# Two small operations of an expert mixture change engines, and its queue of steps starts two steps further on

## The chip, the cores and the metric

The kernel runs on one core of a Trainium2 chip. Its time is the device time of one execution in microseconds (us); of the kernel before, ten executions took 3360.54 to 3378.72 us, and their median, 3370.7 us, is the number that the change is held against. Every engine (PE for matrix products, DVE the vector engine, ACT the scalar engine, POOL the GpSimd engine, SP which only issues transfers) works through its own instructions strictly in the order in which they were written, and engines wait for one another on semaphores.

## What is computed

Two transformer layers over x of shape 4 x 1024 x 128 (four rows of 1024 tokens), float32. The first layer adds two attentions to x; it is not touched by the change. The second layer, cut to what matters:

```python
xn = _layernorm(x)
# linear (random feature) attention, one row of 1024 tokens at a time
x = x + attn(xn) \
# mixture of 8 experts, top 2 of them for each token, and one shared expert for all tokens
for e in range(8):
    h = gelu(xf @ w1[e] + b1[e])               # 128 -> 512
    out = out + combine[:, e:e+1] * (h @ w2[e] + b2[e])
shared = gelu(xf @ ws1 + bs1) @ ws2 + bs2
x + (out + shared)
```

`combine` holds, for each token, the two weights of the softmax over its two best experts.

## The kernel before

**The second layer's stage.** It begins at 2893 us of the execution and lasts to the end, 470 us. It has four strands of work, written as Python generators whose pieces are put one behind the other by a driver loop (line 1811 on):

- *The attention of a row*: `favor_keys(b)` and `favor_queries(b)`, for row b = 0 to 3. In each pass of the loop one piece of each running generator is written. There are 20 passes with the keys of row 0, then three times 40 passes with the queries of one row and the keys of the next, then 20 with the queries of row 3.
- *aside*, the last row's own way into the mixture (`last_row`, line 1350): the layernorm of row 3 (line 215), the router, the tables of blocks, and 16 scatters by POOL (line 1343) that send row 3's tokens, 128 at a time, to their experts' slots in `sorted_x` in HBM. Rows 0 to 2 did this during the first layer.
- *The shared expert* (`shared`, line 1653), in chunks of 512 tokens, 8 in all. One chunk is two pieces. In the first piece: four products `ph` with `ws1` (line 1693) and their Gelu on ACT (line 1697), then the transpose `yT` of the chunk ahead (line 1681), added to x by DVE. In the second: `cT` (line 1660), `py` with `ws2` (line 1669) and with the biases (line 1672).
- *The experts* (`experts`, line 1706): 39 blocks of 256 slots, j = 0 to 38. SP loads the block's rows `xg` from `sorted_x` and its weights `w1`, `w2` (three buffers each). PE transposes the rows (`xgT`, line 1728), DVE copies them out of PSUM (line 1730). `whose` is a copy of the two numbers that ride behind each row, its token's number and its weight (line 1732). PE multiplies by `w1` (`pb`, line 1740), ACT takes the Gelu (`hb`, line 1746), PE multiplies by `w2` (`pe`, line 1755). The result is multiplied by the slot's weight into `yb` (line 1761), and POOL adds it to the tokens' rows of two sums in HBM, by an indirect transfer (line 1765).

The shared expert's first six chunks, then the rest of *aside*, then the experts, then the shared expert's last two chunks make one generator, `fill`. The driver takes a piece of *fill* by a clock of its own: `due` grows by a rate in each pass (0.84 in the first 20, then 0.5, at last 1.2), and for each whole 1 in it a piece of *fill* is written. Two pieces are one chunk of the shared expert or one block of the experts. *aside* gets three pieces of every pass at first, then two, so that it has run dry before *fill* comes to it.

```python
for _ in run(*its):
    for _ in range(3 if taken < 15 else 2):
        next(aside, None); taken += 1
    due += rate
    while due >= 1.0:
        due -= 1.0
        next(filler, None)
```

PE and SP keep the order in which the pieces are written. DVE, ACT and POOL are put in order by the framework's scheduler in this stage.

**The end.** When the last block's sums have landed, SP loads both sums (`y`, 16 transfers of 256 KB, line 1832), DVE adds them to x (line 1836), and eight transfers of 256 KB take x out (line 1838).

Of the kernel before, what the change touches and what calls it, by code (L numbers as in the profile page):

```python
# [12 lines left out]
AF = mybir.ActivationFunctionType  # L13
ALU = mybir.AluOpType
# [4 lines left out]
B, T, D = 4, 1024, 128  # L19
# [42 lines left out]
ROW = D + 2  # L62
# [9 lines left out]
def two_layers(ctx: ExitStack, tc: tile.TileContext, a: dict, out: bass.AP):  # L72
    nc = tc.nc
# [12 lines left out]
    def small(name):  # L86
        return banks.tile([P, 512], F32, tag="small", name=name)
# [1618 lines left out]
    def experts():  # L1706
        rows_of = sorted_x.rearrange("(k q p) d -> k p q d", q=MB // P, p=P)
        loaded, seconds, turned, hidden, whose = {}, {}, {}, {}, {}

        def load(j):  # L1710
            at = nc.sync.value_load(block[0:1, 1, j : j + 1], min_val=0, max_val=ME * PER)
            xg = ff.tile([P, MB // P, ROW], F32, tag="xg", name=f"xg{j}", bufs=3)
            nc.sync.dma_start(xg, rows_of[ds(at, 1)].rearrange("o p q d -> p (o q) d"))
            e = nc.sync.value_load(block[0:1, 0, j : j + 1], min_val=0, max_val=ME - 1)
            w1 = ff.tile([P, MH], F32, tag="w1", name=f"w1_{j}", bufs=3)
            nc.sync.dma_start(w1, a["w1"][ds(e, 1)].rearrange("o d m -> d (o m)"))
            loaded[j] = xg, w1

        def load_second(j):
            e = nc.sync.value_load(block[0:1, 0, j : j + 1], min_val=0, max_val=ME - 1)  # L1720
            w2 = ff.tile([P, MHC, D], F32, tag="w2", name=f"w2_{j}", bufs=3)
            nc.sync.dma_start(w2, a["w2"][ds(e, 1)].rearrange("o (c p) d -> p (o c) d", p=P))
            seconds[j] = w2

        def turn(j):
            pt = small(f"xgT{j}")
            for q in range(MB // P):
                nc.tensor.transpose(pt[:, ts(q, P)], loaded[j][0][:, q, 0:D], ident)  # L1728
            turned[j] = ff.tile([P, MB], F32, tag="xgT", name=f"xgT{j}")
            nc.vector.tensor_copy(turned[j], pt[:, 0:MB])  # L1730
            whose[j] = ff.tile([P, MB // P, 2], F32, tag="whose", name=f"whose{j}", bufs=6)
            nc.gpsimd.tensor_copy(whose[j], loaded[j][0][:, :, D:ROW])

        def one(j):
            w1, xT = loaded.pop(j)[1], turned.pop(j)
            hT = hidden[j] = ff.tile([P, MHC, MB], F32, tag="hb", name=f"hb{j}")
            for c2 in range(MHC // 2):
                ph = small(f"pb{j}_{c2}")
                for k in range(2):
                    nc.tensor.matmul(  # L1740
                        ph[:, ts(k, MB)], lhsT=w1[:, ts(2 * c2 + k, P)], rhs=xT,
                        start=True, stop=True,
                    )
                for k in range(2):
                    c = 2 * c2 + k
                    nc.scalar.activation(
                        hT[:, c, :], ph[:, ts(k, MB)], AF.Gelu, bias=b1s[:, j, c : c + 1]
                    )

        def two(j):  # L1750
            w2, hT, to = seconds.pop(j), hidden.pop(j), whose.pop(j)
            py = small(f"pe{j}")
            for q in range(MB // P):
                for c in range(MHC):
                    nc.tensor.matmul(  # L1755
                        py[:, ts(q, D)], lhsT=hT[:, c, ts(q, P)], rhs=w2[:, c, :],
                        start=(c == 0), stop=(c == MHC - 1),
                    )
            yb = ff.tile([P, MB // P, D], F32, tag="yb", name=f"yb{j}", bufs=3)
            for q in range(MB // P):  # L1760
                nc.vector.tensor_scalar(
                    yb[:, q, :], py[:, ts(q, D)], to[:, q, 1:2], None, ALU.mult
                )

                nc.gpsimd.indirect_dma_start(
                    out=sums[q][:, :],
                    out_offset=bass.IndirectOffsetOnAxis(
                        ap=to[:, q, 0:1].bitcast(I32), axis=0
                    ),
                    in_=yb[:, q, :], in_offset=None, compute_op=ALU.add,  # L1770
                )

        for j in range(NBLK + 3):
            if j < NBLK:
                load(j)
            if 0 <= j - 1 < NBLK:
                turn(j - 1)
            if 0 <= j - 1 < NBLK:
                load_second(j - 1)
            if 0 <= j - 2 < NBLK:  # L1780
                one(j - 2)
                yield
            if 0 <= j - 3 < NBLK:
                two(j - 3)
                yield
# [13 lines left out]
    def fill():  # L1799

        yield from shared(0, SOON)
        for _ in aside:
            pass
        yield from experts()
        yield from shared(SOON, B * T // TC)

    filler = fill()
    due, taken = 0.0, 0
    for k, (rows_now, rate) in enumerate((
        ((0,), 0.84), ((0, 1), 0.5), ((1, 2), 0.5), ((2, 3), 0.5), ((3,), 1.2),  # L1810
    )):
# [88 lines left out]
```

## Time and profile before

| what | value |
|---|---|
| ten runs, median (lowest to highest) | 3370.7 us (3360.54 to 3378.72) |
| the profiled execution, its own time | 3365.59 us |
| its span, from first to last instruction | 3363.8 us |
| mean granted clock of PE over the span | 0.974 |
| busy in the span: PE, DVE, ACT, POOL | 94%, 72%, 55%, 56% |
| `yb` (line 1761), DVE, 78 instructions | 24.1 us |
| `whose` (line 1732), POOL, 39 instructions | 28.8 us |
| loads of ACT's function tables for Exp and Gelu at lines 1392, 1746 and 1697 | 31, 32 and 5, 1283 ns each |

The profiled execution is one of the faster ones: it took 5.1 us less than the median. Times below are in microseconds from the start of its span. In the views a line reads: start, duration, engine, line of the kernel, operation, output <- inputs, shapes, how many instructions were merged, and in brackets how long the engine had been idle and what ended that. PEld is PE's loading of the stationary operand, SPq is SP's queue of transfers.

### The profile page before, as it was taken

To read this page: it belongs to the slowest core of one execution; us is meant where nothing else is said; L and a number is where in the kernel's file an instruction comes from. 1 tells how busy PE (TensorE), PEld (TensorE's weight loads), DVE (VectorE), ACT (ScalarE), POOL (GpSimd) and SP (SyncE) were. 2 spreads that over 40 slices of the span, in tenths; PEclk is the share of its full clock that TensorE was granted. 3 is DMA by queue.
4 is the path that set the end of the run, shared out by engine and by line. 5 is a ranking of instruction groups with operands and counts; after the bars stand their busy time and mean duration, and the time that the engine had idled before them with its cause. 6 is when DMAs were issued, how large, how long until landed. Compare 5 with 4: busy or idle time off the path is not lost. (4 is left out here: it accounts for less than half of the span.)

```text
span 3363.8 us, 48933 instructions
## 1 busy us (share of the span) xinstructions
PE 3172.1 (94%) x15323; PEld 1716.4 (51%) x15323; DVE 2418.7 (72%) x4670; ACT 1850.9 (55%) x3273; POOL 1894.0 (56%) x2345
## 2 busy tenths in 40 slices
PE   6889999999999999999899999999999999889998
PEld 3344444555545444455454455455455554457776
DVE  6787786767778867666867786667666654658886
ACT  3345555555555555555555555555556566246665
POOL 2455555666557666665476666665767654123333
PEclk8899999999999999999999999999999999889999
DMA  5124443433322323333233232332333220024446
GB/s 154 35 82 132 132 140 104 120 101 91 92 69 78 93 80 93 90 93 88 61 91 90 86 94 84 92 89 80 96 90 94 82 84 15 12 62 89 86 88 134
DMA packets 458696, 299.77 MB, mean 89 GB/s; under 512 B 42490, under 2 KB 431108, under 8 KB 458436
## 3 DMA queue, kind: packets, MB, share of 16 engines
q1 hardware_dynamic: 412692, 225.32, 23.9%
q0 software_dynamic: 42976, 70.26, 8.0%
q8 instruction: 122, 2.00, 0.2%
q10 hardware_dynamic: 2768, 1.07, 0.1%
q14 instruction: 138, 1.13, 0.1%
HBM read 179.83 MB, written 116.26 MB: 88 GB/s over the span
## 5 line engine op out<-in xcount | busy, mean ns | idle before, releaser
L620 DVE TENSOR_REDUCE nmh<-mx 128x1 f32<-128x512 f32 x1024 | 664.0, 680 | 293.4 <-PE mx L614 201.4
L874 POOL DMA_INDIRECT sorted_v<-xv,gates x464 | 461.8, 995 | 334.8 <-DMA sorted_v<-xv,gates 249.5
L675 ACT ACTIVATE pT<-sT 128x512 f32<-128x512 f32 x1024 | 557.8, 600 | 162.6 <-PE sT L668 67.5
L955 DVE TENSOR_REDUCE nms<-ps 128x1 f32<-128x1024 f32 x256 | 310.6, 1213 | 259.4 <-ACT ps L953 249.1
L950 PE MATMUL ss<-xnT,qTs 128*128 128x512 f32 x1024 | 491.7, 602 | 3.9 <-ACT qTs L820 2.3
L826 POOL TENSOR_TENSOR g_o<-g_o 128x256 f32<-128x256 f32 x256 | 191.5, 748 | 513.2 <-DVE g_o L825 484.4
L1003 PE MATMUL po<-ow,cTs 128*128 128x512 f32 x1024 | 476.9, 598 | 2.4 <-DVE nmh L620 1.6
L982 PE MATMUL cp<-pTs,vs 128*128 128x512 f32 x1024 | 458.5, 601 | 18.2 <-DVE pTs L974 9.8
L953 ACT COPY ps<-ss 128x512 f32<-128x512 f32 x512 | 298.6, 588 | 216.5 <-PE ss L950 183.9
L957 ACT ACTIVATE ps<-ps,nms 128x1024 f32<-128x1024 f32 x256 | 294.5, 1150 | 146.6 <-DVE nms L955 122.8
L1007 DVE TENSOR_TENSOR g_o<-po,go 128x512 f32<-128x512 f32 x512 | 332.7, 680 | 38.9 <-PE po L1003 18.5
L614 PE MATMUL mx<-ks,qs 72*128 72x512 bf16 x1024 | 313.4, 383 | 17.1 <-DVE nmh L620 7.1
L668 PE MATMUL sT<-qs,ks 75*128 75x512 bf16 x1024 | 311.4, 384 | 8.6 <-DVE nmh L620 3.0
L982 PEld LDWEIGHTS cp<-pTs,vs 128*128 128x128 f32 x1024 | 192.0, 192 | 242.5 <-issue 226.6
L970 PE MATMUL pTp<-ident,ps 128*128 128x128 f32 x2048 | 275.8, 278 | 21.4 <-ACT ps L957 8.8
L970 PEld LDWEIGHTS pTp<-ident,ps 128*128 128x128 f32 x2048 | 243.8, 143 | 90.3 <-issue 21.1
L950 PEld LDWEIGHTS ss<-xnT,qTs 128*128 128x128 f32 x1024 | 189.5, 191 | 183.2 <-issue 108.6
L926 POOL DMA_INDIRECT vs<-yv,gates x232 | 229.0, 987 | 67.5 <-issue 59.7
L926 POOL DMA_INDIRECT yg<-yv,gates x232 | 224.6, 968 | 73.7 <-issue 73.4
L1003 PEld LDWEIGHTS po<-ow,cTs 128*128 128x128 f32 x1024 | 180.0, 192 | 162.8 <-issue 133.7
L987 ACT COPY cTs<-cp 128x512 f32<-128x512 f32 x64 | 37.5, 586 | 392.2 <-PE cp L982 312.6
L658 PE MATMUL ov<-pT,va 128*32 128x512 f32 x2048 | 249.2, 604 | 0.0
(321 smaller groups left out, 4827.1 us busy)
## 6 DMA issues: line engine op xcount, KB each, us to landing
vb<-in_v_w_dram SPq DMA_DIRECT2D x667, 64.0 KB
xs<-sorted_v SPq DMA_DIRECT2D x145, 256.0 KB
yv<-xs SPq DMA_DIRECT2D x145, 256.0 KB
w<-in_w_dram SPq DMA_DIRECT2D x78, 256.0 KB
sorted_x<-nobody SPq DMA_DIRECT2D x16, 1040.0 KB
ow<-in_o_w_dram SPq DMA_DIRECT2D x32, 512.0 KB
qs<-qd SPq DMA_DIRECT2D x144, 64.0 KB
sorted_v<-xv,gates POOLq DMA_INDIRECT x464
```

The costliest lines, as they stand in the source:

```text
L614: nc.tensor.matmul(sc, lhsT=qs[0:NPAIR, i, ts(n, P)], rhs=ks[0:NPAIR, ts(kc, 512)], start=True, stop=True,)
L620: nc.vector.tensor_reduce(halves[:, i, n, kc : kc + 1], sc, axis=AX.X, op=ALU.max)
L668: nc.tensor.matmul(sc, lhsT=ks[:, ts(kt, P)], rhs=qs[:, i, ts(c, 512)], start=True, stop=True,)
L675: nc.scalar.activation(pT, sc, AF.Exp)
L874: nc.gpsimd.indirect_dma_start(out=sorted_v[u % 4][:, :], out_offset=bass.IndirectOffsetOnAxis(ap=column(u, k, n).bitcast(I32), axis=0), i ...
L926: nc.gpsimd.indirect_dma_start(out=to[:, n, :], out_offset=None, in_=unit[u, "y"][:, :], in_offset=bass.IndirectOffsetOnAxis(ap=column(u, ...
L950: nc.tensor.matmul(sc, lhsT=qT[:, ts(n, P)], rhs=xnT[b][:, ts(c, 512)], start=True, stop=True)
L955: nc.vector.tensor_reduce(nm, p, axis=AX.X, op=ALU.max, negate=True)
L970: nc.tensor.transpose(pt[:, ts(k, P)], p[:, ts(4 * k4 + k, P)], ident)
L982: nc.tensor.matmul(cp, lhsT=v[:, kt, :], rhs=pT[:, kt, :], start=(kt == 0), stop=(kt == NT - 1),)
L1003: nc.tensor.matmul(po, lhsT=cT[:, ts(qt, P)], rhs=unit[u, "ow"][:, ts(c, 512)], start=True, stop=True,)
L1007: nc.vector.tensor_tensor(g[:, ts(c, 4), :], po.rearrange("p (e c) -> p e c", e=4), bcast(go[:, ts(c, 4)], P), ALU.mult,)
```

## The change

`whose` is copied by DVE instead of POOL; the product with the slots' weights is made by ACT (a Copy with a scale read from memory, one per partition) instead of DVE; and the driver's clock starts at 2.0 instead of 0.0.

```diff
@@ turn(j)
-            nc.gpsimd.tensor_copy(whose[j], loaded[j][0][:, :, D:ROW])
+            nc.vector.tensor_copy(whose[j], loaded[j][0][:, :, D:ROW])
@@ two(j)
             for q in range(MB // P):
-                nc.vector.tensor_scalar(
-                    yb[:, q, :], py[:, ts(q, D)], to[:, q, 1:2], None, ALU.mult
+                nc.scalar.activation(
+                    yb[:, q, :], py[:, ts(q, D)], AF.Copy, scale=to[:, q, 1:2]
                 )
@@ the driver
     filler = fill()
-    due, taken = 0.0, 0
+    due, taken = 2.0, 0
```

With `due` at 2.0, two more pieces of *fill* are written in the first pass, and *fill* stays two pieces ahead of the attention and of *aside* from then on. On PE the order of the head becomes `kp` (the keys' first product), then the first chunk's `ph`, `cT` and `py`, then `v1p` and the transposes `lnT` of row 3's layernorm; before, `v1p` and the first `lnT` stood ahead of that chunk's `ph`. In the attention of rows 0 to 2, from the second row's keys on, PE's order is as before, with the block's number one higher.

## Prediction

> **What bounds the kernel now.** I read the page's busy shares first, then PE's waits in the head of the last stage (2893.80 to 3017.20, from the keys' first product `kp` of row 0 to that of row 1), the timeline there, and the busy times of two stretches of a later row. The change touches only the last stage.
>
> ```profile
> PE 3172.1 (94%) x15323; PEld 1716.4 (51%) x15323; DVE 2418.7 (72%) x4670; ACT 1850.9 (55%) x3273; POOL 1894.0 (56%) x2345
> ```
>
> PE is the busiest by far, so what counts is where PE waits. The next fence has busy times of PE, PEld, DVE, ACT and POOL in three stretches, then clock, DMA share and GB/s.
>
> ```profile
> 2893.80:3017.20 123.40, 103.74 (x530) 57.29 (x531) 70.88 (x190) 48.98 (x62) 22.10 (x32) 0.86 0.15 41
> 3106.30:3163.00 56.70, 49.82 (x364) 37.46 (x360) 52.34 (x98) 37.70 (x44) 20.61 (x18) 0.97 0.38 79
> 3163.00:3198.60 35.60, 35.34 (x369) 30.28 (x368) 25.52 (x70) 22.71 (x36) 15.88 (x16) 1.00 0.53 111
> ```
>
> In the head PE idles 19.7 us of 123.4. A row's first 57 us are near DVE's bound (52.34 of 56.70, PE idle 6.9); its last 36 us are PE's alone (idle 0.3). The head's waits (total, times, longest):
>
> ```profile
> PE lnT L241 <- DVE xn L234: 6.0, 2, 3.3
> ...
> PE xgT L1728 <- DMA xg<-sorted_x: 3.0, 2, 2.0
> PE lnT L241 <- issue: 2.5, 1, 2.5
> ```
>
> and the timeline of what stands in a row there:
>
> ```profile
> 2908.99 6.30 PE L1693 MATMUL ph<-xnT,ws 128*128 128x512 f32 x8
> 2919.07 1.90 PE L285 MATMUL router<-gw,xnT 128*128 128x8 f32 x16
> 2949.45 2.15 DVE L1330 TENSOR_SCALAR xlast<-x,mv,rstd 128x128 f32<-128x128 f32 x8
> 2994.74 0.97 POOL L1343 DMA_INDIRECT sorted_x<-xlast,at_slot  x1 [1.57 <-DMA sorted_x<-xlast,at_slot]
> 2997.23 0.43 SPq L1713 DMA_DIRECT2D xg<-sorted_x  x1
> 2999.62 0.55 PE L1728 MATMUL xgT<-ident,xg 128*128 128x128 f32 x2 [0.98 <-DMA xg<-sorted_x]
> ```
>
> The reader is to see one chain: router (2919.07), tables, `xlast`, 16 scatters by POOL that each wait for the one ahead, the first expert's load, its transpose. From the router to that load it takes 78.2 us, and no work of PE shortens it. PE needs the shared expert's chunks to fill these 78 us, and they just suffice: it waits 3.0 us for `xg`.
>
> **The driver's clock: the head.** Two pieces ahead is one chunk ahead. On PE the chunk's `ph`, `cT` and `py` and the second chunk's `ph` now stand ahead of the router; before, only the first `ph` did. What stands ahead of the router after the change, from the first `ph` on: `ph`, `cT` 1.04, `py` 3.70 and its bias 1.12, `v1p` 2.02, four `lnT` 0.60, the second `ph` 3.60, `yT` 0.60, `dg` 1.85, `qp` 1.96, `lnT` 0.60, all from the rows of the same timeline. The first `ph` can start when the weights `ws1` are there. SP issues that load at 2898.36; an expert's rows take 2.3 us from issue to landing (2997.23 to 2999.54), I take 2.8 for the larger weights: 2901.2. Its duration: 6.30 in the row above, at a granted clock of 0.50, 3.60 in the rows of a busy PE; I take 5.5, nearer to the cold one, since PE has just waited. So the router starts at 2901.2 + 5.5 + 1.04 + 3.70 + 1.12 + 2.02 + 0.60 + 3.60 + 0.60 + 1.85 + 1.96 + 0.60 = 2923.8, and about 0.3 us of small joints makes 2924.1: **5.0 us later** than 2919.07. With a warm `ph` it is +3.1; with a cold one and 0.2 for a wait on the Gelu, +6.0. The whole chain of scatters moves by this. What hides part of it is already in the sum: the 6.0 and 2.5 us that `lnT` waited are filled.
>
> The Trainium skill has a rule that bears on the 5.5 ("TensorE: Matmul & The Clock Gate", Part 1, What's actually happening): the budget is about 3.4 us of time at half clock, not a number of products. By it a first `ph` after an idle stretch does 1.7 of its 3.60 us of work in those 3.4 us and the other 1.9 at full speed: 5.3, my estimate, which would put the router at +4.8. The row's 6.30 at a clock of 0.50 is dearer than the rule, as it was cold for nearly all of its length.
>
> **What is late next.** SP, in order, holds the load of `xg` until the scatters are done, at 2997.23 + 5.0. PE has one chunk less to do behind the router (3.60 + 1.04 + 3.70 + 1.12 + 0.60 = 10.1), so it idles: its wait ahead of `xgT`, 3.0 us before, becomes some 13 us. Then PE runs one more expert block ahead of row 1's `kp`: `xgT` 0.44, `pb` 1.89, `pe` 1.95, that is **+4.3**. The keys' chain of row 0 (`stab`, `mk`, `va`), which used to run under it, and a half-speed start behind 13 us of idling, add **+1.4** (`pb` takes 3.62 there against 1.89 later, 1.7 more; I take most of it). So `kp` of row 1 goes from 3017.2 to about 3027.9, +10.7.
>
> **`whose` on DVE, `yb` on ACT: the rows.** DVE gives up 0.61 us per block (two `yb`, overlapping), ACT takes them, POOL gives up a copy, DVE takes it.
>
> ```profile
> L1761 DVE TENSOR_SCALAR yb<-pe,whose 128x128 f32<-128x128 f32 x78 | 24.1, 344 | 19.7 <-PE pe L1755 8.1 <-POOL whose L1732 6.7 <-issue 4.7
> L848 ACT ACTIVATE gv<-pv,gates 128x128 f32<-128x128 f32 x96 | 27.4, 369 | 47.5 <-PE pv L836 17.3 <-POOL x L1013 9.1 <-DVE plan L525 8.6
> L1732 POOL COPY whose<-xg 128x4 f32<-128x4 f32 x39 | 28.8, 739 | 9.7 <-DMA xg<-sorted_x 9.7
> L1282 DVE COPY upto<-nb 128x8 f32<-128x8 f32 x1 | 0.2, 173 | 0.0
> ```
>
> The second row is the nearest for ACT's `yb`: the same form, from PSUM, with a scale per partition: 369 ns, two 0.74. The last is the nearest for DVE's `whose`, 173 ns; between 60 (the smallest fills) and 414 (a copy of another shape) I take 0.2. A row has some ten blocks in 91 us (`kp` starts at 3017.2, 3108.5, 3198.8, 3289.6), six of them in the DVE-bound stretch, so DVE sheds 6 × 0.41 = 2.5 us there. Only part of that is time: PE's waits in a row are `pe` or `pb` behind DVE's `xgT` and `kE` (2.1 and 1.8 us), but also behind ACT (1.1), and ACT now has 0.74 more per block in front of the exponentials that the same chain needs. I take a quarter, **−0.7 per row, −2.0** for three. Ends: −6.0 per row (rival two) and +3.0 (rival three). Behind ACT's new wait for `pe` stand the next exponential and `hb`; PE's `qt` and next `pe` wait for these. Copy brings no function table with it, by the order of the loads on ACT (L1746 33 for 32, L1697 4 for 5).
>
> The Trainium skill speaks against the move of `yb`: "ScalarE: Activation LUTs", What ACT_TABLE_LOAD costs, puts an ACTIVATE at 186 ns, 93 more for each pointer operand, and 0.833 ns per element, an estimate of 386 ns for 128 elements with a scale. The row has 369, and DVE's own 344, so by either figure the move makes the product itself slower and is worth something only where DVE is late.
>
> **The tail.** One block fewer is left behind `fo_0`: −4.2 (`xgT` 0.44, `pb` 1.89, `pe` 1.87). But `fo_1` now stands behind the second of the last chunks' `ph`, and `ot_1` behind the last `py`. So DVE's chain from `ot_1` (`nr` 0.18 twice, its reciprocal 0.55, `o` 0.86, in all 1.7, and up to two of the additions of `y`, 0.6 each, in front) has no work of PE left over it: +2.9. In all **−1.3**. The loads of `y` start at 3337.10 behind the last scatter and end at 3351.47; a little earlier changes nothing while the additions to x end last (3357.86 and 2.62 us).
>
> **Sum.** +5.0 + 4.3 + 1.4 − 2.0 − 1.3 = **+7.4**. Against the profiled execution, 3365.59 (span 3363.8), that is 3373.0; it lies 5.1 under the median, so against 3370.7 it is 3378.1. I predict **3378**.
>
> **Rivals.** *One, the head's idle time swallows the chunk* (less than 0.2%): the router is 3.1 late, cold clock adds nothing, the tail keeps its whole −4.2: 3.1 + 4.3 + 0 − 2.0 − 4.2 = +1.2, 3372. For it: the 8.5 us of `lnT` waits. Against: a cold `ph`.
> *Two, faster: DVE sets the rows.* DVE runs in order, and PE's waits there are DVE's. Each row gives back 10 × 0.41 = 4.1 us, and DVE's wait for POOL's `whose` (once a row, 1.9), 6.0; three rows −18. With the head and tail as forecast, 9.4: −8.6, 3362. It decides from 14 us in three rows on. For it: 52.34 of 56.70. Against: in the other stretch PE idles 0.3, and six blocks hold 2.5 of it.
> *Three, ACT becomes late.* In about four of a row's blocks ACT stands in a full stretch with its table loads (1283 ns each); each `yb` there pushes an exponential 0.74 back: 4 × 0.74 × 3 = +9, 3387. For it: ACT is in order, and the exponentials are in PE's chain. Against: 37.70 of 56.70 busy.
> *Four, the change not as said*: a Copy that calls for a table. The order shows none; it gets no chance of its own.
>
> **How the numbers follow.** 0.2% (6.7 us) is about what a measurement of this kernel can tell. Forecast 0.42: its own spread (3375 to 3382) straddles 3377.4, 0.30 over it and 0.12 within. One 0.12, two 0.21, three 0.25. So faster 0.21, same 0.24, slower 0.55. The range takes in three (3387, with 2 for ACT's dearer row) and reaches down to two: 3360 to 3389. The likeliest case's own is 3375 to 3382.
>
> **What would show it.** Router at about 2924; the wait ahead of the first `xgT` 10 us or more; row 1's `kp` near 3028; rows of 90 us; PE's last `o1w` exposed behind `ot_1`. Wrong is the forecast if rows shrink by 4 us or more (two), grow by 3 with PE's waits at ACT (three), or if the first `xgT` comes no later than before, or if the scatters shorten.

## The result and the profile after

The changed kernel took 3392.71 us in the median of ten runs (3383.19 to 3398.41), the kernel before 3371.24 in 34 runs: a ratio of 1.0062, 95% interval 1.0050 to 1.0073. It is slower by 21.5 us. The forecast was 3378 (3360 to 3389): the direction was right, the size too small by a factor of three, and the time lies outside the range.

The profiled execution of the changed kernel took 3394.7 us, its span is 3392.9. The first layer, which the change doesn't touch, is 5.9 us longer in it (the stage begins at 2899.68, before at 2893.80), so the stage is compared from its own start: 470.0 us before, 493.2 after, **+23.2**. Two points divide the stage: the *head* is from `kp` of row 0 to `kp` of row 1 (after the change it holds one expert block more), the *rows* from there to the first `fo` of row 3's queries (the same 2353 instructions of PE in the same order in both kernels), and the *end* is what is left (one block less).

| part | before | after | difference | forecast |
|---|---|---|---|---|
| head | 123.40 | 132.96 | +9.6 | +10.7 |
| rows | 298.00 | 312.41 | **+14.4** | −2.0 |
| end | 48.60 | 47.85 | −0.75 | −1.3 |

The page's busy times, after:

```profile
PE 3185.2 (94%) x15323; PEld 1731.2 (51%) x15323; DVE 2403.8 (71%) x4631; ACT 1872.6 (55%) x3351; POOL 1884.9 (56%) x2306
```

PE has the same 15323 instructions and is busy 13.1 us longer; DVE is relieved by 14.9, as the change says. The three stretches that answer to those of before (columns as there: length, busy PE, PEld, DVE, ACT, POOL, clock, DMA share, GB/s), after:

```profile
2899.68:3032.64 132.96, 104.05 (x555) 59.74 (x556) 71.89 (x195) 51.61 (x70) 24.74 (x32) 0.86 0.17 44
3125.32:3186.10 60.78, 53.20 (x363) 41.96 (x360) 49.89 (x92) 40.92 (x54) 15.65 (x11) 0.88 0.33 72
3186.10:3223.14 37.04, 36.57 (x370) 31.08 (x369) 23.93 (x65) 25.23 (x45) 17.25 (x12) 0.97 0.53 108
```

In the stretch that was near DVE's bound, DVE has 2.45 us less to do, just as forecast, and the stretch is 4.1 us *longer*. The clock fell from 0.97 to 0.88 there. The whole rows, before and then after:

```profile
3017.20:3315.20 298.00, 276.40 (x2353) 222.72 (x2351) 249.11 (x529) 202.44 (x263) 119.77 (x104) 0.97 0.44 91
```

```profile
3032.64:3345.05 312.41, 285.79 (x2353) 232.39 (x2351) 234.76 (x494) 221.04 (x330) 107.04 (x69) 0.93 0.41 86
```

The same 2353 instructions take PE 9.4 us more (285.79 against 276.40), at a clock of 0.93 instead of 0.97, and PE idles 5.0 us more (26.6 against 21.6). These two numbers are the loss of the rows. Where PE waits, in the timeline behind `kp` of one row, before:

```profile
3118.70 1.96 PE L1365 MATMUL qp<-xnT,Wq1T 128*128 128x512 f32 x4
3122.76 2.05 PE L1755 MATMUL pe<-w,hb 128*128 128x128 f32 x16 [2.10 <-DVE xgT L1730]
...
3139.60 0.44 PE L1728 MATMUL xgT<-ident,xg 128*128 128x128 f32 x2 [1.12 <-ACT qfT L1558]
```

and after:

```profile
3137.84 1.10 PE L1365 MATMUL qp<-xnT,Wq1T 128*128 128x512 f32 x2
3141.52 2.08 PE L1365 MATMUL qp<-xnT,Wq1T 128*128 128x512 f32 x2 [2.57 <-DVE xgT L1730]
3143.39 3.62 PE L1755 MATMUL pe<-w,hb 128*128 128x128 f32 x16
...
3162.38 0.41 PE L1728 MATMUL xgT<-ident,xg 128*128 128x128 f32 x2 [1.74 <-issue]
```

Both times PE waits for DVE's copy of `xgT`, which ends at nearly the same distance from `kp` (PE goes on 14.4 us behind it before, 14.2 after). Before, all four products of `qp` were done by then and only `pe` waited. After, two of them stand behind the wait. In the program of before both halves of `qp` wait for a PSUM bank that ACT frees; in the changed one the second half waits for one that DVE frees. The framework hands out the banks. e2 below, with `yb` alone on ACT, has the same wait, and e1 and e3, without it, don't; that the framework goes by what it expects to be freed next is inferred. Then the two products run at half clock (2.08 against 1.10 for the two ahead of them), and so does `pe`: 3.62 against 2.05. In the record of the clock it is at half from 3140.34 to 3147.17.

At the second wait, of 1.74, the view names nobody (`issue`). PE's load of the stationary operand for this `xgT` waited on a semaphore of DVE, which rose at 3162.28, when the first quarter of DVE's `kE` was done; before, the same `xgT` waited for ACT's `qfT`. `pb`, right behind, could go on at 3162.51, when ACT's second `qfT` was done, so both engines end this wait within 0.3 us. It is no longer than before: at `xgT` and the `pb` behind it PE waits 5.5 us in the three rows, before 6.0. ACT's timeline there, before:

```profile
3129.61 1.57 ACT L1746 ACTIVATE hb<-pb,b1s 128x256 f32<-128x256 f32 x4
3131.20 1.28 ACT L1392 ACT_TABLE_LOAD   x1
3137.16 1.91 ACT L1392 ACTIVATE qE<-qE 128x2048 f32<-128x2048 f32 x1 [4.68 <-DVE qE L1390]
```

and after:

```profile
3151.35 1.57 ACT L1746 ACTIVATE hb<-pb,b1s 128x256 f32<-128x256 f32 x4
3157.68 0.63 ACT L1761 ACTIVATE yb<-pe,whose 128x128 f32<-128x128 f32 x2 [4.76 <-PE pe L1755]
3158.33 1.28 ACT L1392 ACT_TABLE_LOAD   x1
3159.62 1.91 ACT L1392 ACTIVATE qE<-qE 128x2048 f32<-128x2048 f32 x1
```

Before, the load of the Exp table ran in ACT's idle time and the exponential waited for DVE alone. After, `yb` stands between the two: ACT waits 4.76 us for `pe`, and the load of 1.28 us comes only then. Little of it is lost time: DVE's `qE`, which the exponential needs, was done at 3159.29, so the exponential starts 0.3 us late. In the third row it is 0.03, in the first 1.36, as much as before.

What grew most is a wait further on, of the keys' product `ddk` for ACT's `hb`, here in the same row:

```profile
3183.35 1.13 PE L1380 MATMUL ddk<-bd,kT 32*128 32x256 f32 x10 [1.85 <-ACT hb L1746]
```

In all rows these waits of `ddk` take 6.3 us, before 0.6 (and 0.6 at `ot`); in return 2.2 us are gone that `pb` waited for DVE's `kE` in this part of the rows. ACT is in a full stretch there, with seven loads of function tables from 3163 to 3183 (before, seven from 3141 to 3161), and `yb` (0.64 us at 3171.10) now stands in it.

In the head, PE's waits after:

```profile
PE xgT L1728 <- DMA xg<-sorted_x: 15.9, 2, 13.9
PE ph L1693 <- DMA ws<-in_ws_dram: 5.5, 1, 5.5
```

The 13 us in front of the first `xgT` are there, and the `lnT` waits have given way to a wait for `ws1`. In the end, `oT1p` waits for DVE's chain, as the prediction's tail had it:

```profile
3383.53 1.09 PE L1603 MATMUL oT1p<-ident,o 128*128 128x128 f32 x4 [3.35 <-DVE o L1593]
```

### The profile page after: what moved, and what is told of

Same layout as the page of the kernel before. It is cut to its first block, busy times and chain, and to the rows that moved or that the text cites. A ratio compares the mean times of both kernels' runs of the same rounds, so it can differ in the third digit from the quotient of the medians.

```text
span 3392.9 us, 48952 instructions
## 1 busy us (share of the span) xinstructions
PE 3185.2 (94%) x15323; PEld 1731.2 (51%) x15323; DVE 2403.8 (71%) x4631; ACT 1872.6 (55%) x3351; POOL 1884.9 (56%) x2306
## 3 DMA queue, kind: packets, MB, share of 16 engines
q14 instruction: 137, 1.12, 0.1%
## 5 line engine op out<-in xcount | busy, mean ns | idle before, releaser
L982 PE MATMUL cp<-pTs,vs 128*128 128x512 f32 x1024 | 457.9, 600 | 17.1 <-DVE pTs L974 9.7
L953 ACT COPY ps<-ss 128x512 f32<-128x512 f32 x512 | 298.6, 588 | 218.5 <-PE ss L950 185.4
L1765 POOL DMA_INDIRECT sum<-yb,whose x78 | 122.7, 1573 | 234.3 <-ACT yb L1761 201.7
```

Source lines behind the costliest of these rows:

```text
L982: nc.tensor.matmul(cp, lhsT=v[:, kt, :], rhs=pT[:, kt, :], start=(kt == 0), stop=(kt == NT - 1),)
```

## The experiments

Fourteen kernels were run in four batches. Ratios are against the kernel before on the same chip; the chips differ (before: 3338.5, 3337.8, 3336.2 and 3368.9 us in the four batches), so times are compared within a batch or by ratios. Head, rows, PE's busy and idle time in the rows, its clock there, and the end come from one profiled execution of each, in us.

| kernel | ratio (95%) | head | rows | busy | idle | clock | end |
|---|---|---|---|---|---|---|---|
| before | 1 | 123.4 | 298.0 | 276.4 | 21.6 | 0.97 | 48.6 |
| after | 1.0062 (1.0050, 1.0073) | 133.0 | 312.4 | 285.8 | 26.6 | 0.93 | 47.9 |
| e1: clock at 2.0 alone | 1.0031 (1.0019, 1.0044) | 130.9 | 298.6 | 276.5 | 22.1 | 0.97 | 47.8 |
| e2: `yb` alone | 1.0015 (1.0006, 1.0024) | 123.1 | 302.2 | 276.2 | 26.0 | 0.97 | 48.6 |
| e3: `whose` alone | 1.0020 (1.0011, 1.0028) | 126.6 | 297.8 | 275.3 | 22.5 | 0.97 | 49.4 |
| e4: `yb` and `whose` | 1.0046 (1.0032, 1.0059) | 129.4 | 309.0 | 283.5 | 25.5 | 0.93 | 48.8 |
| e5: after, `dg` twice | 1.0049 (1.0035, 1.0062) | 133.8 | 305.2 | 285.9 | 19.2 | 0.95 | 47.4 |
| e6: e4, first `whose` on POOL | 1.0033 (1.0020, 1.0045) | 121.2 | 307.8 | 281.7 | 26.1 | 0.94 | 49.2 |
| e7: after, four of ten `yb` on DVE | 1.0039 (1.0025, 1.0052) | 132.7 | 300.8 | 275.7 | 25.1 | 0.97 | 47.1 |
| e8: clock at −2.0 alone | 1.0001 (0.9991, 1.0010) | 114.9 | 298.7 | 278.0 | 20.7 | 0.96 | 54.9 |
| e9: clock at 2.0 and `yb` | 1.0054 (1.0041, 1.0066) | 131.7 | 305.2 | 279.9 | 25.4 | 0.95 | 47.4 |
| e10: e2, `v1p` of row 1 twice | 1.0033 (1.0022, 1.0045) | 122.7 | 312.4 | 285.6 | 26.8 | 0.93 | 48.8 |
| e11: e4, `v1p` of row 1 twice | 1.0052 (1.0040, 1.0065) | 127.1 | 312.3 | 285.0 | 27.2 | 0.93 | 48.8 |
| e12: clock at −2.0, 2.0 back in row 2 | **0.9978** (0.9969, 0.9986) | 117.5 | 298.9 | 279.0 | 19.9 | 0.97 | 48.6 |
| e13: after, `yb` 2, 3 on DVE | 1.0033 (1.0020, 1.0047) | 132.0 | 305.5 | 280.4 | 25.1 | 0.95 | 47.9 |
| e14: after, `yb` 4, 5 on DVE | 1.0050 (1.0029, 1.0071) | 130.9 | 307.7 | 279.8 | 27.9 | 0.96 | 47.9 |

### The parts alone

The theory after the result (A) was that `yb` on ACT costs the rows, and the driver's clock the head; the rival (B), that the shift by two pieces costs both. The three edits, each on the kernel before: the first alone is e1, the second (with ACT's call in place of DVE's) e2, the third e3, and the second and third together e4.

```diff
-    due, taken = 0.0, 0
+    due, taken = 2.0, 0
...
-                    yb[:, q, :], py[:, ts(q, D)], to[:, q, 1:2], None, ALU.mult
+                    yb[:, q, :], py[:, ts(q, D)], AF.Copy, scale=to[:, q, 1:2]
...
-            nc.gpsimd.tensor_copy(whose[j], loaded[j][0][:, :, D:ROW])
+            nc.vector.tensor_copy(whose[j], loaded[j][0][:, :, D:ROW])
```

e1, expected:

> Only the driver's clock at 2.0; yb stays on DVE, whose on POOL. Theory A (the slots' weights on ACT cost the rows): the stage's head is longer by what the changed kernel shows, 133.0 against 123.4 us from the keys' first product of row 0 to that of row 1, +9.6; the rows keep the 90 to 91 us of before and the end gives nothing or a little back, so +7 to +10 us in all. Theory B (the driver's shift cost the rows too, since block and attention meet in another phase): rows of 94 to 96 us and +20 us or more.

Measured: head +7.5, rows +0.6, end −0.8. Rival B falls: the clock at 2.0 costs the head alone, about half of the whole loss (0.0031 of 0.0062).

e2, expected:

> Only yb on ACT; clock at 0.0, whose on POOL. Theory A: the head as before within 2 us, rows of 94 to 96 us as in the changed kernel, +11 to +15 us in all. Theory B: rows as before, within 3 us of no change.

Measured: rows +4.2, a third of what theory A had. The waits were those of the changed kernel (2.57 at `qp`, 1.74 at `xgT`), but PE's busy time did not grow:

```profile
3082.43:3174.39 91.96, 83.81 (x719) 68.05 (x718) 71.02 (x143) 65.50 (x98) 33.21 (x31) 0.96 0.41 87
```

e3, expected:

> Only whose on DVE. Theory A: DVE takes 0.17 us more for a block where it is late in six blocks of a row; one or two of those reach PE: 0 to +3 us. A rival, that DVE's copy waits for the load of xg ahead of work that PE needs and so costs the rows: +5 us or more.

Measured: nothing in the rows (−0.25). The loss, 4.8 us by the medians, is by the profile in the head (+3.2), and not in the rows, where the rival had it. e4, expected:

> Yb on ACT and whose on DVE, clock at 0.0. Theory A: as with yb alone, +11 to +15 us, rows of 94 to 96 us, since the yb on ACT is the cause; the copy on DVE adds less than 2 us. If the parts add up, this and the driver's clock alone together give the +21 us of the whole change.

Measured: rows +11.0, so in the rows the two parts together cost more than their sum (4.2 − 0.25). Over the whole kernel e1 and e4 (0.0031 and 0.0046) add up to the change's 0.0062 within the intervals. A row of e4 with the waits of e2:

```profile
3087.05:3182.07 95.02, 87.44 (x719) 71.09 (x718) 72.27 (x153) 65.57 (x98) 31.15 (x21) 0.91 0.41 85
```

Idle time is nearly that of e2 (7.6 against 8.2), but the same 719 instructions take 87.44 instead of 83.81, at a clock of 0.91 instead of 0.96. The waits alone don't make the loss; the granted clock does the rest.

### What the copy on DVE costs in the head

In e4, DVE's timeline in the head shows the copy in front of work that doesn't need it:

```profile
2956.68 0.27 DVE L1472 TENSOR_REDUCE top<-mxT 16x1 f32<-16x128 f32 x1
2969.06 0.17 DVE L1732 COPY whose<-xg 128x4 f32<-128x4 f32 x1 [12.11 <-DMA xg<-sorted_x]
2969.14 0.21 DVE L1474 TENSOR_SCALAR each<-ident,top 16x16 f32<-16x16 f32 x1
2969.27 0.67 DVE L1665 COPY cTs<-cT 10x512 f32<-10x512 f32 x1
```

The first `whose` waits 12.11 us for the load of `xg`; `cTs` of the last chunk, ready long before, stands behind it, and PE waits for `cTs`:

```profile
2970.00 2.07 PE L1672 MATMUL py<-cTs,bias 10*128 10x512 f32 x2 [9.25 <-DVE cTs L1665]
```

e6 takes that wait away:

```diff
-            nc.vector.tensor_copy(whose[j], loaded[j][0][:, :, D:ROW])
+            (nc.gpsimd if j < 4 else nc.vector).tensor_copy(whose[j], loaded[j][0][:, :, D:ROW])
```

Expected:

> Clock at 0.0, yb on ACT, whose on DVE from the fifth block on, the first four on POOL. In the run with all of whose on DVE, DVE stood up to 12 us in front of the first copy, which waits for the load of xg, with the copy cTs that PE's last chunk needs behind it. If that is what the head lost: the head falls back to 123 to 125 us from 129.4, and the kernel is 4 to 7 us faster than with all of whose on DVE. If the head was longer by a late scatter alone: no change of the head's cTs wait and less than 2 us. Theory C adds: should the rows begin at another place of the clock's stretches, they may also fall from 95.5 to 92 us, a further 7 to 10 us.

Measured: the wait of 9.25 is gone and the head is 121.2, for 129.4 in e4 (by the ratios of the whole, 1.0033 for 1.0046, some 4 us). Not all of the 8.2 us are the copy's: the scatters of e4 also took longer (one waited 3.77 us for the one ahead, where the others waited 1.6 to 2.9). `xg` had landed when DVE copied it at 2969.06, and PE turned it at 2973.71, 4.6 us later; so much the copy cost in e4 at least. The rows stayed long (307.8). In the changed kernel the last chunk was long done when DVE stood there, so the copy cost it less: its head is 2.0 us over that of e1. Whether these 2.0 are the copy's isn't shown: the five kernels with the clock at 2.0 and `whose` on DVE (after, e5, e7, e13, e14) have heads of 130.9 to 133.8 us, and that of e1 is 130.9.

### The clock and the waits

e5 adds work. With b the row and k = 0 for the keys:

```diff
-            for n in range(NT):
+            for n in [*range(NT)] * (2 if b and k == 0 else 1):
                 nc.tensor.matmul(
                     dps[:, ts(n, NH)], lhsT=sq[:, ts(n, P)], rhs=hsum, start=True, stop=True
                 )
```

Expected:

> The changed kernel, with the eight keys' products dg of rows 1 to 3 computed twice (the second time over the first): 1.85 us more work for PE in each row, just ahead of the 2.6 us in which PE waits for DVE's copy of xgT in the middle of qp. Theory C: what the rows lose is mostly the granted clock, which goes to half for two stretches of 3.4 us behind that wait; with the wait filled by 1.85 us of work the clock stays up, so the rows shrink from 95 us to 91 to 93 although work was added, and the kernel is 6 to 12 us faster than the changed one. Theory A (waits alone): the added work only fills the wait, the rows stay at 95 us within 0.5, and the time of the changed kernel stands within 2 us. If PE's work is the bound: +1.85 us per row.

Measured: three times 1.85 us more work, and the rows are 7.2 us shorter than those of the changed kernel (305.2 against 312.4). PE's idle time falls by 7.4; without the added 5.6, its busy time falls from 285.8 to 280.4. So the work in the gap was free, and some 5 us of the clock came back, but not all of them. A as stated (no shorter rows) falls. C fits in part; but the rows also begin at other places against the clock's stretches here, and e9 and e10 show that this alone can change as much.

e9 to e11 ask whether `whose` is needed for the dear rows (some 95 us where cheap ones take 92) (D) or whether it depends on where the rows fall against the clock's stretches (E). e10 and e11:

```diff
-            for n in range(4):
+            for n in [*range(4)] * (2 if b == 1 else 1):
                 nc.tensor.matmul(
                     ps[:, ts(n, P)], lhsT=xnT[b][:, ts(4 * q + n, P)], rhs=w1a["Wv1T"],
                     start=True, stop=True,
                 )
```

e9, expected:

> The clock at 2.0 and yb on ACT; whose stays on POOL. PE's waits in the rows should be those of yb on ACT alone (2.6 us at qp, 1.7 at xgT). With yb alone the rows took 92.0 us, with whose on DVE too 95.3, with the same waits but twice as much time at half clock. Theory D (the copy on DVE is needed for the dear rows): rows of 92 us here, +10 to +13 us against the kernel before. Theory E (which of the two a kernel gets depends on where the rows begin against the stretches of 3.4 us in which the clock is granted, and whose has no part in it): rows may be 95.5 us here as well, +17 to +22 us.

e10, expected:

> Yb on ACT alone, and the products v1p of row 1's keys computed twice: 1.95 us more of PE's work, once, after which the rows 2 and 3 begin at another place of the clock's stretches. Theory E: the rows behind it can fall into the dear state, 95.5 us each instead of 92, so +5 to +10 us against yb alone, more than the added 1.95. Theory D: rows of 92 us as with yb alone, and +0 to +2 us against it.

e11, expected:

> Yb on ACT and whose on DVE, clock at 0.0, and the products v1p of row 1 computed twice, as in the run beside it. Theory E: the rows behind may fall into the cheap state, 92 us each, so the kernel is up to 6 us faster than without the added work. Theory D: 95.5 us as before it, +0 to +2 us against the kernel without the added work.

Measured: e9 has a dear and a cheap row in one execution, with nearly the same waits in each (the idle times are 7.6 and 8.2 us):

```profile
2997.44:3092.41 94.97, 87.38 (x719) 71.17 (x718) 71.10 (x143) 65.62 (x98) 33.34 (x31) 0.91 0.40 85
3092.41:3184.38 91.97, 83.80 (x718) 68.08 (x717) 71.05 (x143) 65.57 (x98) 33.41 (x31) 0.96 0.41 87
```

A stretch at half clock doesn't always follow a wait. In the dear row (the first line) a `pe` runs mostly at half clock 12.6 us after PE's last wait; ahead of it stand the small products `dg`, `vsum` and `ddq`. In the cheap row the same `pe`, behind the same products, doesn't:

```profile
3024.23 3.62 PE L1755 MATMUL pe<-w,hb 128*128 128x128 f32 x16
3117.86 2.05 PE L1755 MATMUL pe<-w,hb 128*128 128x128 f32 x16
```

And e10, `yb` alone with 1.95 us of work added once, has rows of 312.4 instead of 302.2: 8.3 us more than the added work. D falls: dear rows come without `whose` on DVE. E is borne out as far as an early shift turns cheap rows into dear ones; the other way, from dear to cheap, it did not happen (e11 stayed dear). What decides it in each row was not found. Dear rows came only with `yb` on ACT: without it (before, e1, e3, e8) PE is busy for 275.3 to 278.0 us in the rows, with all of it there (after, e2, e4, e6, e9) for 276.2 to 285.8.

### Which of the two waits

e7, e13 and e14 put `yb` back on DVE for some blocks of the changed kernel, by the last figure of their number: 2, 3, 4, 5 in e7 (as shown), 2 and 3 in e13, 4 and 5 in e14.

```diff
+                if j % 10 in (2, 3, 4, 5):
+                    nc.vector.tensor_scalar(
+                        yb[:, q, :], py[:, ts(q, D)], to[:, q, 1:2], None, ALU.mult
+                    )
+                else:
+                    nc.scalar.activation(
+                        yb[:, q, :], py[:, ts(q, D)], AF.Copy, scale=to[:, q, 1:2]
+                    )
```

e7, expected:

> The changed kernel, but yb stays on DVE for the blocks whose number ends in 2, 3, 4 or 5, which lie in the stretch of a row where ACT changes its function table twice a block; six of ten are on ACT. Theory A': yb costs where ACT stands in front of it waiting for pe, with the load of the Exp table (1.28 us) and the exponential behind it, and where it changes which PSUM bank the second half of qp gets. Then the waits of 2.6 us at qp and 1.7 us at xgT go, rows return to 90 to 92 us, and the kernel is 9 to 14 us faster than the changed one. Rival: ACT's load as such counts, and the rows keep most of the loss (94 us or more).

Measured: rows of 91.4 and 91.9 us, PE busy 275.7, clock 0.97. By the clock and PE's busy time that is the kernel before, though 60% of `yb` are on ACT. The waits at `qp` and `xgT` are those of before; of those of `ddk` for `hb`, 1.85 us remain in two of the rows. By the time of the whole, 1.0039, it is where e1 is (1.0031), within the intervals: what is left is mostly the head's (+9.3; the rows +2.8). The profiled execution was the fastest of its five, 5.9 us under their median. The gain of 9 to 14 us that was expected on the changed kernel is 11.6 in the profile's rows, and 0.0023 (some 8 us) by the ratios.

e13, expected:

> The changed kernel with yb on DVE for the blocks whose number ends in 2 or 3: the second half of qp gets a bank that ACT frees again, while ACT's yb of the blocks ending in 4 and 5 still stands in front of the load of the Exp table. If the wait in the middle of qp makes the loss: it is gone, pe waits 2.1 us behind a whole qp as before the change, and rows take 90 to 92.5 us. If the table load makes it: the wait of 1.7 us at xgT stays and rows take 93.5 to 96.

e14, expected:

> The changed kernel with yb on DVE for the blocks whose number ends in 4 or 5: ACT loads the Exp table early again, while the second half of qp still gets a bank that DVE frees. If the wait in the middle of qp makes the loss: 2.6 us there stay and rows take 93.5 to 96 us. If the table load makes it: the 1.7 us at xgT fall to 1.1 with a name of ACT's qfT, and rows take 90 to 92.5 us. If each has a part: 92 to 94 us in both runs.

Measured: in e13 `pe` waits 2.1 us behind a whole `qp`, the 1.74 at `xgT` stay, and the rows take 305.5. In e14 the 2.6 in `qp` stay, `xgT` waits for `qfT` as before the change (2.45, 1.13 and 1.12), and the rows take 307.7. With both waits as in the changed kernel they take 312.4, with neither (e7) 300.8. PE's busy time lies between, too (280.4 and 279.8). That fits a part for each, but doesn't show it: e2 has both waits, and PE is busy for 276.2 us, less than in either, so where the rows fall against the clock can have made these differences. In e14 PE idles 27.9 us, more than in any other, so the change at `xgT` saved no idle time; the table load as a cause is not shown.

### The other direction of the clock

e8 starts the driver at −2.0, on the kernel before. Expected:

> The kernel before, with the driver's clock starting at -2.0: one chunk behind instead of one ahead, the first chunk behind the router. If the chain from the router to the scatters sets the head, the router comes about 6 us earlier (the 6.3 us of the first ph no longer stand ahead of it), the chunk's work fills time that PE waited in, and the head is 4 to 8 us shorter; the block that is moved to the end costs 0 to 4 us there. In all -8 to 0 us against the kernel before. Rival: what is moved to the end costs all that the head gains, +0 to +5 us.

Measured: the head is 8.5 us shorter, and the end 6.3 longer (one block more stands there); no difference in the time. e12 gives the two pieces back before the end:

```diff
-    due, taken = 0.0, 0
+    due, taken = -2.0, 0
...
+        due += 2.0 * (k == 2)
```

Expected:

> The kernel before, with the driver's clock at -2.0 in the head and 2.0 added to it where the keys of row 2 start, so that the end is that of the kernel before. In the run with -2.0 throughout, the head was 8.5 us shorter (114.9 against 123.4) and the end 6.7 longer (171.9 against 165.2). Here the head should keep its 8.5, the row with the added block should take 4.3 us more (xgT, pb, pe), and the end 165: -3 to -5 us against the kernel before. Rival: the block costs more than its work where it is put in, or the end stays long, and nothing is gained.

Measured: 3327.97 against 3336.15 us, ratio 0.9978 (0.9969 to 0.9986): 8.2 us faster than the kernel before, and the fastest of all. In its profile the stage takes 464.9 us, 5.1 less than before, about what was expected, but by other parts; the other 3 us of the medians lie ahead of the stage or in the spread between executions. Its head:

```profile
2859.80:2977.26 117.46, 100.21 (x504) 55.50 (x505) 69.64 (x187) 45.90 (x57) 20.20 (x30) 0.85 0.12 35
```

PE idles 17.3 us of it (before: 19.7), and no wait for `xg` is left among PE's waits: the chunk that was moved behind the router covers the scatters. The head gains 5.9 us and not 8.5: PE is busy for 100.2 us in it, in e8 for 96.0 with the same work, at a clock of 0.85 against 0.88. The row with the added block is 4.0 us longer, as expected (4.3), but the two behind it are 2.1 and 1.0 shorter than before; why was not followed further.

## Why the prediction was wrong

**The head was right, in its mechanism and nearly in its size.** `ph` started 7.4 us behind `kp`, as worked out from the load of `ws1`, and took 5.93 (5.5 taken). The router came 3.8 us later and not 5.0: the durations that were added up overlap by some 0.1 to 0.2 us at each joint. From there to the first `xgT` it took 80.4 us, before 80.5: the chain is rigid. PE's wait in front of it was 13.9 us (13 forecast). From `xgT` to `kp` it was 5.9 us more (4.3 + 1.4 forecast). e1, with the driver's clock alone, has 7.5 of these 9.6 us. Two small readings of the prediction were off: the clock of 0.50 beside the `ph` of 6.30 is that of its first 5 us (0.57 over the whole), and 3289.6 is not a start of `kp`. No term rests on either.

The estimate of 5.3 for `ph`, worked out from the 3.4 us of the Trainium skill ("TensorE: Matmul & The Clock Gate", Part 1, What's actually happening), was below the 5.93 of the trace.

**The end was right**: −0.75 for −1.3, with the exposed chain where it was foreseen (3.35 us of waiting at `oT1p`).

**The rows failed**, in the step "I take a quarter, −0.7 per row". It measured +3.6, +5.5 and +5.3. DVE did shed its 2.5 us, but its copy of `xgT`, for which PE waits, came only 0.3 us earlier behind `kp`; the reductions `vs` (3.68 us) and `mq` (2.47) stand ahead of it in both kernels. So the relief was worth next to nothing. `yb` alone (e2) brings 4.2 of the 14.4 us, all of it idle time of PE; the rest is time at half clock. Three things cost time that the prediction had not priced.

- The price of ACT's `yb` was taken as its duration, 0.74 for a block. In the trace the pair takes 0.63. What it brought is waits: ACT stands up to 4.76 us for `pe` in front of it, and in ACT's full stretch PE's `ddk` waits for `hb` (6.3 us over the rows, 0.6 before). The prediction named the exponential and `hb` behind `yb`, and gave the waits no price. Rival three had the engine (+9 in the rows, measured +14.4), but not the kind of loss: the larger part is the clock's, so it is in part luck that its number came near.
- The change of an engine also changed the banks, and put the wait for DVE in the middle of `qp` (2.6 us for 2.1 in each row). The program's waits on PE show this without a run. The prediction had read the order of the instructions and not what each waits for.
- The clock. 5.0 of the 14.4 us are waits (26.6 against 21.6 of idle time); 9.4 are the same instructions with more time at half clock (44.4 us of the rows in the record of the clock, before 17.1). The prediction priced a cold clock in the head and nowhere else.

Rival two, DVE as the rows' bound, fell with the stretch that grew while DVE's work shrank. Rival one fell with the head. Rival four fell with the counts of the page: DVE has 39 instructions less and ACT 78 more.

## What to carry to other kernels

An instruction that moves to another engine brings its waits with it: look at what stands behind it there in order. When a scheduler or a pool decides, compare also what each instruction waits for, and not only the order. Work that only fills a rigid chain's time belongs behind the chain's start, and can be given back later (e12).

## What the runs showed of the hardware

Behind the wait of 2.6 us shown, PE ran at a granted clock of 0.50 (5.5 us of that row). With such waits the same instructions cost between nothing (e2) and 9.4 us more in three rows, by where they fall: PE's busy time for one set of instructions went from 275.3 to 285.8 us over these kernels. Not each stretch at half clock follows a wait (e9). In the record of the clock, its stretches at half speed last 3.4 us or multiples of that, but for the last, with which the execution ends. The Trainium skill ("TensorE: Matmul & The Clock Gate", Part 1, What's actually happening) speaks of a free-running window of about 3.4 us whose activity sets the clock; these lengths agree with it. On ACT the load of the Exp table stood directly in front of the exponential, so the Copy that waited 4.76 us ahead of it held it back; in the row shown 0.3 of its 1.28 us were lost by that. On POOL the copy of 128 x 4 numbers took 739 ns on average, on DVE 198 in e3; the kernel with the shorter instruction was the slower one.
